# A re-costed order for the first pass of a Mamba-style block, with x_proj's weights filled up to a full 128 x 128

## The chip, the cores and the metric

The kernel runs on one core of a Trainium2 chip. The metric is the device time of one execution in microseconds. Before the change it is 10,700.71 us, the median of three runs (10,697.7 to 10,703.4). The profile used here is of one execution whose span is 10,692.9 us.

## The reference, cut to what matters

Input `x` is 8 images of 64 x 64 tokens with 96 channels (L = 4096 tokens each). The first layer is a group norm and a selective-scan block; after it come a linear attention and a quantized feed-forward layer. What the change touches is all ahead of the scan:

```python
xz = einsum('bhwc,ec->bhwe', group_norm(x), in_proj_w)         # 96 -> 192 + 192 channels
xin, z = split(xz, 2)
xc = silu(conv3x3_depthwise(xin) + conv_b)                     # 192 channels, 64 x 64
x_hw, x_wh = xc.reshape(b, 192, L), xc.transpose(0, 1, 3, 2).reshape(b, 192, L)
xs = stack([x_hw, x_wh, flip(x_hw), flip(x_wh)])               # 4 directions
x_dbl = einsum('bkdl,kcd->bkcl', xs, x_proj_weight)            # 192 -> 6 + 16 + 16 per direction
dts, Bs, Cs = x_dbl[:, :, :6], x_dbl[:, :, 6:22], x_dbl[:, :, 22:]
delta = softplus(dt_w @ dts + dt_bias);  y = selective_scan(xs, delta, A, Bs, Cs)
```

The forward and the flipped direction of one reading order share their input, so one product with 2 x 38 = 76 output rows serves both.

## The kernel before, in words

The program is three passes, one after the other, with tensors in memory between them.

**Pass 1** (`pass1`) takes the images in four pairs. For each image, `statistics` loads x in groups of 512 tokens, transposes it on TensorE (4 transposes of 128 tokens) and collects means on VectorE. `group_norm` makes the scale from two tiny matmuls with `gmat`. `projection` loads and transposes the group again, normalizes it on VectorE (`xn`), and multiplies it by three weights of 96 rows x 128 columns (`pa`); ScalarE copies the results to the padded images `xpad` and applies SiLU to the gates `z`. `convolution` does the nine taps of the depthwise 3 x 3 convolution on VectorE over 128 x 4096 elements. 192 channels are no multiple of 128, so a pair makes three convolutions: channels 0 to 127 of each image, and one tile with the last 64 channels of both images (rows 0 to 63 of the first, 64 to 127 of the second). They run in the order 0, 2, 1. ScalarE then writes SiLU once in transposed order (`ut`, stored to `u_d`) and once in place (`u`).

`x_projection(b, o, q)` multiplies 512 positions of an image by `w_xp`. With o = 0 the positions are adjacent in `u`; with o = 1 they are read in the transposed order, 64 elements apart. Each unit has two matmuls that add in one PSUM tile: 128 rows of the image's own tile, then the 64 rows which belong to the image in the shared one. Each fp32 matmul shows as two passes in the trace, so a unit is four passes. 128 units make up the pass. ScalarE (or VectorE, for half of the last pair's groups) evacuates 76 x 512 to `xd`, and SyncE's queue stores it. `split` reads part of that back, cuts it into three bf16 parts by turns of a ScalarE cast and a GpSimd subtraction, and stores them for pass 2. There are six such units per image.

**Pass 2** does the scans, and **pass 3** the rest. The change leaves both as they are.

What sets the order: `weave` holds a list of generators. Each one yields the engine that its next instructions go to, a cost, a delay until the result is there, and where it matters a set of buffers (`Slots`). `weave` always takes the piece that can begin first by these numbers, and emits its instructions. `InOrder` then keeps each engine, SyncE's DMA queue too, in exactly that order. The costs put no wait into the program; they only choose the order. An instruction whose data is late holds up everything behind it on its engine. All instructions emitted through `InOrder` carry line 89 in the profile, so they are told apart by tile names.

Of the kernel before, what the change touches and what calls it, by code (L numbers as in the profile page):

```python
# [33 lines left out]
F32 = mybir.dt.float32  # L34
# [5 lines left out]
PSUM = bass.MemoryType.PSUM  # L40
DRAM = bass.MemoryType.DRAM

P = 128
NB, HH, WW, C = 8, 64, 64, 96
L = HH * WW
DI, N, R, K = 192, 16, 6, 4
# [27 lines left out]
def load_by_type(queue, dst, src):  # L74

    queue.dma_start(dst[:, 0], src[0:P])
    queue.dma_start(dst[0:64, 1], src[P:DI])
    queue.dma_start(dst[64:P, 1], src[P:DI])
# [154 lines left out]
def pass1(ctx, tc, g, consts, ident, mhalf, engines, u_d, z_d, xd_d, b_d, dt_d):  # L233
# [8 lines left out]
    four = ctx.enter_context(tc.tile_pool(name="p1four", bufs=4))  # L242
    ps_tr = ctx.enter_context(tc.tile_pool(name="p1tr", bufs=2, space=PSUM))
    ps_mm = ctx.enter_context(tc.tile_pool(name="p1mm", bufs=3, space=PSUM))
    ps_px = ctx.enter_context(tc.tile_pool(name="p1px", bufs=2, space=PSUM))
    ps_one = ctx.enter_context(tc.tile_pool(name="p1ps", bufs=1, space=PSUM))
    Q = GRP // P

    ORDER = (0, 2, 1)
# [9 lines left out]
    act.dma_start(gmat, g["group_mean"])  # L259
    conv_w = wp.tile([P, 2, 9], F32, name="conv_w")  # L260
    conv_b = wp.tile([P, 2, 1], F32, name="conv_b")
    w_xp = wp.tile([P, 2, 2, 2 * NXD], F32, name="w_xp")

    def later_loads():
        load_by_type(act, conv_w, g["conv_w"])
        load_by_type(act, conv_b, g["conv_b"])
        w0 = 0
        for rows in (slice(R, R + N), slice(R + N, NXD), slice(0, R)):
            wide = rows.stop - rows.start
            for k2 in range(2):  # L270
                src = slice(k2 * NXD + rows.start, k2 * NXD + rows.stop)
                load_by_type(act, w_xp[:, :, :, w0 : w0 + wide], g["x_projT"][:, :, src])
                w0 += wide


# [5 lines left out]
        pool.memset(t[:, 1 : HH + 1, WW + 1 : WW + 2], 0.0)  # L281

    sts, gms, us, done = {}, {}, {}, {}
    pts, mms, pxs = Slots(2), Slots(3), Slots(2)
    counts = {}

    def one_more(key, of, end):
# [14 lines left out]
    def statistics(b, q):  # L302
        if b > 1:
            yield "proj", b - 2
        yield "sp", 0.5, 2.0
        x = transposed(three, "xs", b, q)
        next(x)
        yield "pe", 0.7, 0.3, pts
        pt, slot = next(x), pts.taken
        end = yield "dve", 0.7  # L310
        if b not in sts:
            sts[b] = two.tile([C, NG, 6], F32, name="st")
        dve.bn_stats(sts[b][:, q, :], pt[0:C, :])
        pts.release(slot, end)
        one_more(("st", b), NG, end)

    def group_norm(b):

        yield "st", b
        yield "dve", 0.2  # L320
        mv = two.tile([C, 2], F32, name="mv")
        dve.bn_aggr(mv, sts[b].rearrange("p a b -> p (a b)"))
        yield "pe", 0.3
        pm = ps_one.tile([P, 2], F32, name="pm", tag="pm")
        pe.matmul(pm[0:C, 0:1], gmat, mv[:, 0:1], start=True, stop=True)
        yield "dve", 0.5
        gm = wp.tile([C, 2], F32, name=f"gm{b}")
        dve.tensor_copy(gm[:, 0:1], pm[0:C, 0:1])
        dq = two.tile([C, 1], F32, name="dq")
        dve.tensor_sub(dq, mv[:, 0:1], gm[:, 0:1])  # L330
        dve.scalar_tensor_tensor(dq, dq, dq, mv[:, 1:2], ALU.mult, ALU.add)
        yield "pe", 0.3
        pv = ps_one.tile([P, 2], F32, name="pv", tag="pm")
        pe.matmul(pv[0:C, 0:1], gmat, dq, start=True, stop=True)
        yield "dve", 0.2
        dve.tensor_copy(gm[:, 1:2], pv[0:C, 0:1])
        end = yield "pool", 1.0
        pool.tensor_scalar(gm[:, 1:2], gm[:, 1:2], 1e-5, None, ALU.add)
        pool.tensor_tensor(gm[:, 1:2], gm[:, 1:2], mhalf[0:C, 0:1], ALU.pow)
        gms[b] = gm  # L340
        done["stats", b] = end

    def projection(b, q):

        pair, j = b // 2, b % 2
        cols = slice(q * GRP, (q + 1) * GRP)
        rows = slice(1 + q * RPG, 1 + (q + 1) * RPG)
        inner = slice(1, WW + 1)
        own, other = slice(64 * j, 64 * j + 64), slice(64 - 64 * j, P - 64 * j)
        third = xpad[2 + pair % 2]  # L350
        yield "stats", b
        yield "sp", 0.5, 2.0
        x = transposed(four, "xt", b, q)
        next(x)
        if pair > 0:
            yield "conv", pair - 1, j
        if pair > 1:
            yield "conv", pair - 2, 2
        yield "pe", 0.7, 0.3, pts
        pt, slot = next(x), pts.taken  # L360
        end = yield "dve", 0.7
        pts.release(slot, end)
        xn = four.tile([C, GRP], F32, name="xn")
        dve.tensor_scalar(xn, pt[0:C, :], gms[b][:, 0:1], gms[b][:, 1:2], ALU.subtract, ALU.mult)
        def product(w):
            yield "pe", 1.1, 0.3, mms
            p = ps_mm.tile([P, GRP], F32, name="pa", tag="mm")
            pe.matmul(p, w, xn, start=True, stop=True)
            return p, mms.taken

        pa, slot = yield from product(w_in[:, 0:P])
        end = yield "act", 0.6
        act.copy(xpad[j][:, rows, inner], pa.rearrange("p (h w) -> p h w", w=WW))
        mms.release(slot, end)
        pa, slot = yield from product(w_mix[:, j, :])
        yield "act", 0.6
        act.copy(third[own, rows, inner], pa[own, :].rearrange("p (h w) -> p h w", w=WW))
        z1 = three.tile([P, GRP], F32, name="z1")
        end = yield "act", 0.6
        act.activation(z1[other, :], pa[other, :], AF.Silu)  # L380
        one_more(("proj", b), NG, end)
        mms.release(slot, end)
        pa, slot = yield from product(w_in[:, DI : DI + P])
        z0 = three.tile([P, GRP], F32, name="z0")
        end = yield "act", 0.6
        act.activation(z0, pa, AF.Silu)
        mms.release(slot, end)
        yield "sp", 0.9
        sp.dma_start(z_d[b][P:DI, cols], z1[other, :])
        sp.dma_start(z_d[b][0:P, cols], z0)  # L390

    def convolution(pair, c):
# [28 lines left out]
            yield "stored", *before  # L421
        parts = chunk_rows(pair, c)
        for w in (slice(i, i + WW // 4) for i in range(0, WW, WW // 4)):
            yield "act", 1.2
            ut = two.tile([P, L // 4], F32, name="ut")
            act.activation(ut.rearrange("p (w h) -> p h w", h=HH), uv[:, :, w], AF.Silu, bias=conv_b[:, ty, :])
            yield "sp", 0.5
            for part, b, ch in parts:
                sp.dma_start(u_d[b][1][ch, w.start * HH : w.stop * HH], ut[part, :])
        for h in range(2):  # L430
            cols = slice(h * (L // 2), (h + 1) * (L // 2))
            end = yield "act", 1.9
            act.activation(u[:, cols], u[:, cols], AF.Silu, bias=conv_b[:, ty, :])
        done["u", pair, c] = end
        end = yield "sp", 0.5
# [3 lines left out]

    def x_projection(b, o, q):  # L440
        pair, j = b // 2, b % 2
        half = slice(64 * j, 64 * j + 64)
        yield "u", pair, j
        yield "u", pair, 2
        px = None
        for ty, u, part in ((0, us[pair, j], slice(0, P)), (1, us[pair, 2], half)):
            end = yield ("pe", 0.85) if px else ("pe", 0.85, 0.3, pxs)
            if px is None:
                px, slot = ps_px.tile([P, GRP], F32, name="px", tag="px"), pxs.taken
            if o == 0:  # L450
                src = u[part, q * GRP : (q + 1) * GRP]
            else:
                src = u[part, :].rearrange("p (h w) -> p w h", w=WW)[:, q * RPG : (q + 1) * RPG, :]
            pe.matmul(px[0 : 2 * NXD, :], w_xp[part, ty, o, :], src, start=ty == 0, stop=ty == 1)
        one_more(("xproj", b), 2 * NG, end)
        by_dve = pair == NB // 2 - 1 and q % 2 == 1
        end = yield ("dve" if by_dve else "act"), 0.6
        xd = three.tile([2 * NXD, GRP], F32, name="xd")
        (dve.tensor_copy if by_dve else act.copy)(xd, px[0 : 2 * NXD, :])
        pxs.release(slot, end)  # L460
        end = yield "sp", 0.5, 2.5
        sp.dma_start(xd_d[b][o][:, q * GRP : (q + 1) * GRP], xd)
        one_more(("xd", b, o), NG, end)

    def split(b, o, row, rows, pieces, at, dst):

        wide, used = GRP, rows * pieces
        yield "xd", b, o
        yield "sp", 0.5, 2.5
        bq = three.tile([P, wide], F32, name="bq")  # L470
        src = xd_d[b][o][row : row + rows].rearrange("r (s t) -> (r s) t", s=pieces)
        sp.dma_start(bq[0:used], src[:, at : at + wide])
        yield "act", 0.6
        bs = three.tile([P, NS, wide], BF16, name="bs")
        act.copy(bs[0:used, 0, :], bq[0:used])
        yield "pool", 1.2
        pool.tensor_sub(bq[0:used], bq[0:used], bs[0:used, 0, :])
        yield "act", 0.6
        act.copy(bs[0:used, 1, :], bq[0:used])
        yield "pool", 1.2  # L480
        pool.tensor_sub(bs[0:used, 2, :], bq[0:used], bs[0:used, 1, :])
        yield "sp", 0.9
        half = used // 2
        for k2 in range(2):
# [612 lines left out]
```

## Time and profile before

| view | what it gives |
| --- | --- |
| span, busy share | 10,692.9 us; VectorE 90%, ScalarE 87%, GpSimd 86%, TensorE 73% |
| first convolution tap of each pair | 74.8, 240.3, 441.9 and 653.8 us |
| end of the last convolution tap | 859.3 us |
| last x_proj matmul starts | 937.4 us |
| first VectorE instruction of pass 2 | 983.5 us |
| convolution taps in all, VectorE | 96 x 4,590 ns and 12 x 2,531 ns, together 471 us |
| x_proj passes, TensorE | 512, mean 929 ns of one |

From about 1,000 us on, VectorE, ScalarE and GpSimd are all over 90% busy. The first 980 us look otherwise: no engine is busy all the time. A share of busy time over the whole span hides this, so the profile has to be read by stage. [...]how long one really holds the engine is seen from the distance between starts in a dense stretch.

### The profile page before, as it was taken

How to read it: one execution, taken by the hardware profiler on the slowest of the kernel's cores; microseconds unless marked ns; L12 is line 12 of the kernel's file. 1: busy time of each engine (PE TensorE's matmuls, PEld its weight loads, DVE VectorE, ACT ScalarE, POOL GpSimd, SP SyncE). 2: the span in 40 equal slices, each digit the busy share in tenths (PEclk: the TensorE clock that was granted, in tenths of full speed). 3: DMA queues.
4: the chain of work that ended last, by engine and by line, in shares of the span. 5: the costliest groups of instructions: out<-in, count | busy, mean ns of one | idle time of the engine just before them, and what ended most of it. 6: DMA issues, size and time to landing. Idle time of an engine off the chain costs nothing.

```text
span 10692.9 us, 151366 instructions
## 1 busy us (share of the span) xinstructions
PE 7776.9 (73%) x51232; PEld 6178.1 (58%) x51232; DVE 9619.3 (90%) x6982; ACT 9298.7 (87%) x21355; POOL 9181.8 (86%) x3270
## 2 busy tenths in 40 slices
PE   6876777777767777777777777777777777766887
PEld 3222656666656666665656666665565666655766
DVE  6664999999999999999999999999999999997776
ACT  4445999999999999999999999999999999996665
POOL 1324999999999999999999999999999999997886
PEclk8777999998899999999899999988999999897776
DMA  5555666669896666689976766789766667997442
GB/s 145 170 165 168 211 217 216 210 211 204 197 210 215 210 219 213 213 205 203 200 218 210 222 211 214 208 200 204 216 210 215 217 207 214 199 198 184 135 128 59
DMA packets 928009, 2103.22 MB, mean 197 GB/s; under 512 B 274391, under 2 KB 422648, under 8 KB 925700
## 3 DMA queue, kind: packets, MB, share of 16 engines
q1 hardware_dynamic: 919812, 2092.79, 69.6%
q8 instruction: 410, 6.72, 0.3%
q14 instruction: 363, 2.97, 0.1%
q10 hardware_dynamic: 7424, 0.74, 0.1%
HBM read 1917.59 MB, written 175.66 MB: 196 GB/s over the span
## 4 chain that ended last, share of the span: by engine, by line
ACT 28%; DVE 20%; PE 17%; issue 17%; POOL 13%; DMA 4%; SPq 1%; ACTq 0%; DVEq 0%; POOLq 0%
DVE h L89 15%; ACT x L89 13%; ACT da L89 10%; POOL c L89 9%; PE wide L89 6%; PE acc L89 6%; DVE wide L89 3%; PE px L89 2%; PE mm L89 2%; ACT L89 1%; POOL xg L89 1%; PE pa L89 1%; ACT delta L89 1%; DMA xdt<-dt_d 1%; SPq L89 1%
## 5 line engine op out<-in xcount | busy, mean ns | idle before, releaser
L89 POOL TENSOR_TENSOR c<-c,h 128x2048 f32<-128x2048 f32 x1536 | 6965.6, 4549 | 395.8 <-DVE h L89 335.4
L89 DVE TENSOR_TENSOR_SCAN h<-da,carry,wide 128x1024 f32<-128x1024 f32 x2304 | 5253.5, 2331 | 204.4 <-PE wide L89 147.4
L89 ACT ACTIVATE x<-duT,bT 128x128 f32<-128x128 f32 (+1 forms) x14336 | 4155.2, 366 | 63.5 <-PE wide L89 57.5
L89 PE MATMUL acc<-ident,c 128*128 128x128 f32 x24576 | 3480.5, 297 | 546.6 <-POOL c L89 539.6
L89 ACT ACTIVATE da<-delta,a_neg 128x1024 f32<-128x1024 f32 x3072 | 3504.2, 1144 | 345.6 <-DVE h L89 333.9
L89 PEld LDWEIGHTS acc<-ident,c 128*128 128x128 f32 x24576 | 3133.3, 155 | 881.1 <-POOL c L89 747.9
L89 PE MATMUL wide<-ident,x 128*128 128x128 f32 x11264 | 1614.0, 292 | 877.9 <-DVE h L89 861.0
L89 PEld LDWEIGHTS wide<-ident,x 128*128 128x128 f32 x11264 | 1344.9, 149 | 1171.7 <-DVE h L89 509.3
L89 DVE TENSOR_TENSOR_SCAN h<-da,wide 128x1024 f32<-128x1024 f32 x768 | 1707.0, 2270 | 82.8 <-PE wide L89 62.0
L89 DVE TENSOR_TENSOR wide<-du,wide 128x1024 f32<-128x1024 f32 x1216 | 1459.2, 1212 | 156.9 <-PE wide L89 156.8
L89 PE MATMUL wide<-xb,sel 96*128 96x512 bf16 x2432 | 752.4, 394 | 584.9 <-DVE h L89 494.7
L89 POOL TENSOR_TENSOR xg<-duT,bT 128x512 f32<-128x512 f32 (+1 forms) x640 | 891.4, 1408 | 82.3 <-PE wide L89 65.1
L89 PE MATMUL wide<-ident,xg 128*128 128x128 f32 x3584 | 500.2, 285 | 239.6 <-DVE h L89 233.7
L89 PEld LDWEIGHTS <-sel 96*128 96x128 bf16 x2432 | 223.0, 101 | 776.0 <-DVE h L89 387.3
L89 PEld LDWEIGHTS wide<-ident,xg 128*128 128x128 f32 x3584 | 412.6, 146 | 316.0 <-issue 143.9
L89 POOL TENSOR_TENSOR du<-delta,u 128x1024 f32<-128x1024 f32 x192 | 455.0, 2370 | 101.4 <-ACT delta L89 92.2
L89 ACT ACT_TABLE_LOAD x385 | 494.0, 1283 | 6.8
L89 PE MATMUL px<-u,w_xp 128*76 128x512 f32 (+1 forms) x512 | 409.5, 929 | 76.5 <-ACT xd L89 47.8
L89 POOL TENSOR_TENSOR bq<-bq,bs 128x512 f32<-128x512 f32 (+1 forms) x48 | 114.2, 2392 | 401.3 <-ACT bs L89 401.2
L89 DVE SCALAR_TENSOR_TENSOR u<-xpad,conv_w,u 128x4096 f32<-128x4096 f32 x96 | 440.6, 4590 | 1.2
L89 PEld LDWEIGHTS px<-u,w_xp 128*76 128x76 f32 (+1 forms) x512 | 78.8, 190 | 364.4 <-issue 217.2
L89 ACT COPY xd<-px 76x512 f32<-76x512 f32 x112 | 65.2, 583 | 254.8 <-PE px L89 169.9
(130 smaller groups left out, 6224.0 us busy)
## 6 DMA issues: line engine op xcount, KB each, us to landing
c<-xd_d SPq DMA_DIRECT2D x1024, 1024.0 KB
c<-xd_d SPq DMA_DIRECT2D x1024, 512.0 KB
u<-u_d SPq DMA_DIRECT2D x128, 512.0 KB
xdt<-dt_d SPq DMA_DIRECT2D x1152, 36.0 KB
xb<-b_d SPq DMA_DIRECT2D x384, 96.0 KB
u<-u_d SPq DMA_DIRECT2D x128, 256.0 KB
y_d<-y SPq DMA_DIRECT2D x24, 1024.0 KB
y<-y_d SPq DMA_DIRECT2D x64, 384.0 KB
```

Source lines behind the costliest of these rows:

```text
L89: ins = getattr(self.engine, op)(*args, **kwargs).ins
```

## The change

It has three parts, all in pass 1.

1. **x_proj's weights.** `w_xp` becomes 128 rows x 3 x 2 x 128 columns, zeroed at the start by GpSimd. Its first block holds the weights of the 128 own channels; the second and third hold those of the last 64 channels in rows 0 to 63 or 64 to 127, with zeros in the other half. Both matmuls of a unit then use all 128 rows of `u` and write 128 columns, 76 of them used. This is meant to spare TensorE the change between 64 and 128 rows and to show it as fully used.
2. **The plan's durations.** Costs and delays given to `weave` are replaced by those that the author read from a trace: a GpSimd subtraction of `split` 4.4 in place of 1.2 (2.5 for the last image but one), `ut` 2.1 in place of 1.2, a product 0.75 in place of 1.1, loads with a delay of 4.0 in place of 2.0 or 2.5, and small ones.
3. **Buffers and engines.** The two tiny group-norm products use the `mm` PSUM tiles, so that x_proj has three PSUM tiles in place of two. The subtractions of the last image go to VectorE.

```diff
-    ps_px = ctx.enter_context(tc.tile_pool(name="p1px", bufs=2, space=PSUM))
-    ps_one = ctx.enter_context(tc.tile_pool(name="p1ps", bufs=1, space=PSUM))
+    ps_px = ctx.enter_context(tc.tile_pool(name="p1px", bufs=3, space=PSUM))
...
-    w_xp = wp.tile([P, 2, 2, 2 * NXD], F32, name="w_xp")
+    w_xp = wp.tile([P, 3, 2, P], F32, name="w_xp")
+    pool.memset(w_xp, 0.0)
...
-                load_by_type(act, w_xp[:, :, :, w0 : w0 + wide], g["x_projT"][:, :, src])
+                act.dma_start(w_xp[:, 0, :, w0 : w0 + wide], g["x_projT"][0:P, :, src])
+                for j in range(2):
+                    act.dma_start(w_xp[64 * j : 64 * j + 64, 1 + j, :, w0 : w0 + wide], g["x_projT"][P:DI, :, src])
...
-    pts, mms, pxs = Slots(2), Slots(3), Slots(2)
+    pts, mms, pxs = Slots(2), Slots(3), Slots(3)
...
-        yield "sp", 0.5, 2.0
+        yield "sp", 0.6, 4.0
...
-        yield "pe", 0.3
-        pm = ps_one.tile([P, 2], F32, name="pm", tag="pm")
+        yield "pe", 0.3, 0.3, mms
+        pm, slot = ps_mm.tile([P, GRP], F32, name="pm", tag="mm"), mms.taken
...
-            yield "pe", 1.1, 0.3, mms
+            yield "pe", 0.75, 0.4, mms
...
-            yield "act", 1.2
+            yield "act", 2.1
...
-        for ty, u, part in ((0, us[pair, j], slice(0, P)), (1, us[pair, 2], half)):
-            end = yield ("pe", 0.85) if px else ("pe", 0.85, 0.3, pxs)
+        for ty, u in ((0, us[pair, j]), (1 + j, us[pair, 2])):
+            end = yield ("pe", 0.9, 0.4) if px else ("pe", 0.9, 0.4, pxs)
...
-            pe.matmul(px[0 : 2 * NXD, :], w_xp[part, ty, o, :], src, start=ty == 0, stop=ty == 1)
+            pe.matmul(px, w_xp[:, ty, o, :], src, start=ty == 0, stop=ty > 0)
...
-        end = yield "sp", 0.5, 2.5
+        end = yield "sp", 0.9, 3.0
         sp.dma_start(xd_d[b][o][:, q * GRP : (q + 1) * GRP], xd)
...
+        name, cost, by = ("dve", 0.65, dve) if b == NB - 1 else ("pool", 4.4 if b < NB - 2 else 2.5, pool)
         yield "xd", b, o
-        yield "sp", 0.5, 2.5
+        yield "sp", 0.7, 4.0
...
-        yield "pool", 1.2
-        pool.tensor_sub(bq[0:used], bq[0:used], bs[0:used, 0, :])
+        yield name, cost
+        by.tensor_sub(bq[0:used], bq[0:used], bs[0:used, 0, :])
```

More of the change, by code (lines that the diff above doesn't have):

```diff
@@ L322, in group_norm @@
         dve.bn_aggr(mv, sts[b].rearrange("p a b -> p (a b)"))
-        yield "pe", 0.3
-        pm = ps_one.tile([P, 2], F32, name="pm", tag="pm")
+        yield "pe", 0.3, 0.3, mms
+        pm, slot = ps_mm.tile([P, GRP], F32, name="pm", tag="mm"), mms.taken
         pe.matmul(pm[0:C, 0:1], gmat, mv[:, 0:1], start=True, stop=True)
-        yield "dve", 0.5
+        end = yield "dve", 0.5
+        mms.release(slot, end)
         gm = wp.tile([C, 2], F32, name=f"gm{b}")
@@ L331, in group_norm @@
         dve.scalar_tensor_tensor(dq, dq, dq, mv[:, 1:2], ALU.mult, ALU.add)
-        yield "pe", 0.3
-        pv = ps_one.tile([P, 2], F32, name="pv", tag="pm")
+        yield "pe", 0.3, 0.3, mms
+        pv, slot = ps_mm.tile([P, GRP], F32, name="pv", tag="mm"), mms.taken
         pe.matmul(pv[0:C, 0:1], gmat, dq, start=True, stop=True)
-        yield "dve", 0.2
+        end = yield "dve", 0.2
+        mms.release(slot, end)
         dve.tensor_copy(gm[:, 1:2], pv[0:C, 0:1])
@@ L351, in projection @@
         yield "stats", b
-        yield "sp", 0.5, 2.0
+        yield "sp", 0.6, 4.0
         x = transposed(four, "xt", b, q)
@@ L360, in projection @@
         pt, slot = next(x), pts.taken
-        end = yield "dve", 0.7
+        end = yield "dve", 0.8
         pts.release(slot, end)
@@ L431, in convolution @@
             cols = slice(h * (L // 2), (h + 1) * (L // 2))
-            end = yield "act", 1.9
+            end = yield "act", 2.0
             act.activation(u[:, cols], u[:, cols], AF.Silu, bias=conv_b[:, ty, :])
@@ L441, in x_projection @@
         pair, j = b // 2, b % 2
-        half = slice(64 * j, 64 * j + 64)
         yield "u", pair, j
@@ L450, in x_projection @@
             if o == 0:
-                src = u[part, q * GRP : (q + 1) * GRP]
+                src = u[:, q * GRP : (q + 1) * GRP]
             else:
-                src = u[part, :].rearrange("p (h w) -> p w h", w=WW)[:, q * RPG : (q + 1) * RPG, :]
-            pe.matmul(px[0 : 2 * NXD, :], w_xp[part, ty, o, :], src, start=ty == 0, stop=ty == 1)
+                src = u.rearrange("p (h w) -> p w h", w=WW)[:, q * RPG : (q + 1) * RPG, :]
+            pe.matmul(px, w_xp[:, ty, o, :], src, start=ty == 0, stop=ty > 0)
         one_more(("xproj", b), 2 * NG, end)
@@ L475, in split @@
         act.copy(bs[0:used, 0, :], bq[0:used])
-        yield "pool", 1.2
-        pool.tensor_sub(bq[0:used], bq[0:used], bs[0:used, 0, :])
+        yield name, cost
+        by.tensor_sub(bq[0:used], bq[0:used], bs[0:used, 0, :])
         yield "act", 0.6
         act.copy(bs[0:used, 1, :], bq[0:used])
-        yield "pool", 1.2
-        pool.tensor_sub(bs[0:used, 2, :], bq[0:used], bs[0:used, 1, :])
+        yield name, cost
+        by.tensor_sub(bs[0:used, 2, :], bq[0:used], bs[0:used, 1, :])
         yield "sp", 0.9
```

## The prediction

> **What bounds the kernel now.** I read the page first: over the whole span VectorE is busiest (90%), but the change touches pass 1 alone, so I took the busy time of each engine in 100-us stretches. The columns are PE, PEld, DVE, ACT and POOL busy, then the granted clock, the DMA share and GB/s.
>
> ```profile
> 400.00:500.00 100.00, 78.57 (x102) 19.31 (x100) 61.91 (x21) 36.26 (x54) 57.84 (x20) 0.57 0.42 119
> 600.00:700.00 100.00, 78.83 (x105) 16.97 (x104) 56.31 (x16) 33.17 (x48) 44.70 (x18) 0.58 0.47 131
> 900.00:1000.00 100.00, 52.39 (x135) 18.66 (x134) 21.31 (x17) 35.01 (x70) 28.82 (x17) 0.66 0.50 150
> 1000.00:1100.00 100.00, 73.28 (x560) 62.83 (x559) 96.67 (x51) 97.47 (x217) 93.96 (x25) 0.95 0.66 213
> ```
>
> Pass 2 (last line) is full on three engines. In pass 1 none is full; TensorE is the busiest, at a clock that falls to 0.57. Next the waits of the first 960 us, and those of SyncE's queue:
>
> ```profile
> DVE xn L89 <- PE pt L89: 156.0, 32, 31.1
> PE pt L89 <- DMA xt<-in_x: 56.2, 18, 7.6
> PEld px L89 <- ACT xd L89: 92.5, 42, 9.8
> ...
> SPq L89 <- ACT xd L89: 171.5, 69, 6.9
> SPq L89 <- POOL bs L89: 100.2, 18, 14.4
> ```
>
> VectorE waits for TensorE; TensorE for loads and for evacuations; the queue that issues those loads stands up to 14.4 us behind one GpSimd subtraction. The timelines of TensorE and VectorE show it at one place:
>
> ```profile
> 451.78 23.07 PE L89 MATMUL px<-u,w_xp 128*76 128x512 f32 x24 [2.77 <-ACT xd L89]
> 474.78 1.94 PE L89 MATMUL pt<-ident,xt 128*96 128x128 f32 x8
> ...
> 441.92 3.25 DVE L89 TENSOR_SCALAR u<-xpad,conv_w 128x4096 f32<-128x4096 f32 x1
> 475.98 1.59 DVE L89 TENSOR_SCALAR xn<-pt,gm 96x512 f32<-96x512 f32 x2 [30.81 <-PE pt L89]
> ```
>
> VectorE has one tap left to give and then stands 30.8 us, since `xn` is next in its order and its transpose lies behind the x_proj passes. The same recurs at 657 us (31.1 us). So pass 1 is set by order: x_proj's slow stretches on TensorE, with VectorE idle beside them.
>
> [...]from 447 to 474 us PE is busy 24.2 of 27 us, yet the clock is 0.50. A dense stream of 76-column passes does not hold the clock; dense 96x128 products do from 52 to 90 us. [...]adjacent passes of one form at full clock start 0.43 us apart, and 0.52 where 128 and 64 rows change. [...]o = 1 passes (elements 256 bytes apart) start 0.86 us apart even where the clock is 1.00 (919.4 to 922.6 us). [...]Here one GpSimd subtraction takes 1.15 us alone and up to 6.1 us beside the convolution, against 1.2 in the old plan.
>
> **The change, part by part.**
>
> *Weights, row changes.* In `749.19 9.06 ... x18` (full clock, adjacent reads, rows changing) a pass is 9.06/18 = 0.50 us, in the 24 strided passes above 0.96. Without changes 0.43 and 0.86. A strided unit goes from 3.84 to 3.43 us: 64 x 0.41 = 26 us. A plain unit at full clock goes from 2.01 to 1.72: by the single records, 87 of some 250 plain passes run at half clock, about 22 of 64 units, so 42 at full: 42 x 0.29 = 12 us.
>
> *Weights, clock.* The other 22 plain units run at half clock, some 3.7 us each. If full columns and rows count as busy, they fall to 1.72: 22 x 2.0 = 44 us. No row of this trace shows a 128x128 fp32 pass of 512 columns; the bounds are 22 x 0.3 = 7 us (clock unchanged) and 44 us, and I take 44, since 96x128 products hold the clock. Projections gain too: their 384 passes average 0.71 and 0.70 us against 0.59 at full clock, an excess of 45 us, of which I take a third, 15 us. The strided passes gain nothing from the clock, as they are as slow at 1.00 as at 0.50. TensorE in sum: 26 + 12 + 44 + 15 = 97 us of 711 busy before 960 us. Wider weight loads cost nothing: the 128-column loads of `pa` (225 ns for `px`'s 190) lie under the passes before them. Zeroing `w_xp` on GpSimd lies in its idle start (16 us idle until 17.6 us), ahead of the loads issued from 37.9 us on; their number stays 18.
>
> *How much of it reaches the end.* From 230 to 650 us PE is busy 344 of 420 us and VectorE 278, so TensorE sets the pace, and VectorE is the next limit: a convolution of 2.35 + 8 x 4.4 = 37.6 us plus its share of `xn` and statistics, the first two starting 49 and 50 us apart. 47 x 12 = 564 us after 75 us gives about 640 us for the last tap, against 859. The 97 us fit in this gap of 220, so I count them whole.
>
> *Order.* With 4.4 for a subtraction, the casts behind it on ScalarE and the stores behind it on SyncE come later in the order, with `xd` copies and x loads ahead of them. That goes for the 100 us of queue waits on `bs`, and part of the 92.5 us that loads of x_proj wait for `xd`. The third PSUM tile for x_proj helps the latter. From 230 to 860 us PE idles 141 us; I take 55, about half of the queue's wait for `bs`. Bounds: 0 (only other places to wait) and 110. The new waits of `pm` and `pv` for an `mm` tile hold, on TensorE, everything behind them, until ScalarE has evacuated a product (0.6 us each): 16 of them, under 10 us in all, beside VectorE's taps.
>
> *Tail.* From the last tap (859.3) to pass 2's first VectorE instruction (983.5) are 124 us: SiLU 28 with waits, x_proj until 938, then 45 for the last split and pass 2's first loads. After: SiLU 4 x 2.08 + 2 x 2.0 = 12, say 15; 16 units, 8 x 1.72 + 8 x 3.43 = 41; the 45 stay. That is 101, or 23 less, of which half is counted above: 10 us. The last image's 12 subtractions on VectorE, some 0.7 us each by its copies, are not more than on GpSimd.
>
> Sum: 97 + 55 + 10 = 162 us. 10,701 - 162 = 10,539, rounded to 10,540. Passes 2 and 3 stay: their order is planned from a clock of its own.
>
> **The rivals.** *VectorE's floor:* the plan comes out so well that convolutions follow each other at 47 us. Last tap at 640, tail 101: pass 2 starts at 741, 242 us earlier: about 10,450. For it: GpSimd, ScalarE and SyncE all have room. Against: every engine is in fixed order, and load waits of 4 to 8 us remain. *Row changes only:* the clock stays low and the new order only moves waits: 26 + 12 + 7 = 45 and a few us of the tail: 10,650. [...]*A worse order:* the same products, but wrong costs (0.9 for strided matmuls, which take 1.7) let the plan put transposes and group norm behind x_proj; five more holds like that at 442 us, 5 x 31 = 155, less the 97 and 10 that remain, some 48 us slower: 10,750. For it: the plan is blind to o. Against: it was as blind before (0.85).
>
> **How the numbers follow.** Forecast 0.60, VectorE's floor 0.15, row changes only 0.15, a worse order 0.06, and 0.04 for gains and losses that cancel. The range goes from VectorE's floor, 10,450, to just short of the row-change case, 10,640. Faster takes the first three: 0.90; same 0.04; slower 0.06.
>
> **What would show it.** In the changed profile x_proj passes should start 0.43 (plain) and 0.86 us (strided) apart with no 0.52; clock in the stretches 400 to 700 us above 0.75; the wait of `xn` for `pt` well under 156 us; SyncE's wait for `bs` under 50; last tap near 720, pass 2's first VectorE instruction near 820 us. The prediction is wrong if strided passes also speed up, if the clock stays near 0.57, or if `xn` waits longer than before.

## The result and the profile after

The changed kernel takes 10,573.22 us (median, 10,562.6 to 10,580.3) against 10,702.06 us for the kernel before in the same comparison: a ratio of 0.9876, 95% interval 0.9859 to 0.9893. That is 129 us less. The prediction was 10,540 us, 162 us less, with a range of 10,450 to 10,640. The direction and the range hold. The experiments below show that the sum behind it does not: the term for the weights is several times too large, the term for the order half of what the order gave.

All of it comes from pass 1. The first VectorE instruction of pass 2 starts at 853.4 us instead of 983.5, which is 130 us. The busy time in 100-us stretches (PE, PEld, DVE, ACT and POOL busy, then granted clock, DMA share, GB/s), kernel after:

```profile
400.00:500.00 100.00, 91.17 (x229) 36.20 (x228) 78.67 (x36) 68.59 (x96) 55.31 (x14) 0.98 0.73 234
600.00:700.00 100.00, 63.88 (x117) 22.05 (x118) 90.76 (x25) 59.42 (x70) 63.59 (x17) 0.83 0.62 204
```

VectorE has gone from 62 to 79 us in the stretch from 400 us and from 56 to 91 in the one from 600 us; the clock there rose from 0.57 and 0.58 to 0.98 and 0.83. The waits of the first 840 us (waiter, releaser, us in total, times, longest):

```profile
DVE xn L89 <- PE pt L89: 58.3, 23, 11.4
PE pt L89 <- DMA xt<-in_x: 19.3, 12, 4.5
PEld px L89 <- ACT xd L89: 39.5, 31, 5.7
```

and those of SyncE's queue in the same time:

```profile
SPq L89 <- ACT xd L89: 180.7, 77, 8.9
SPq L89 <- POOL bs L89: 17.6, 9, 3.8
```

`xn` waits 58 us for its transposes instead of 156, and SyncE's queue 18 us for GpSimd's subtractions of the split instead of 93 in the same 840 us (100 in the first 960; another 9 us now go to the subtractions that VectorE does). The long hold at the start of a pair, 30.8 us before, is still there but shorter, 11.4 us. TensorE and VectorE after, at the same point of the third pair:

```profile
388.99 22.39 PE L89 MATMUL px<-u,w_xp 128*128 128x512 f32 x28
411.20 1.05 PE L89 MATMUL pt<-ident,xt 128*96 128x128 f32 x8
...
398.15 2.35 DVE L89 TENSOR_SCALAR u<-xpad,conv_w 128x4096 f32<-128x4096 f32 x1
411.93 1.52 DVE L89 TENSOR_SCALAR xn<-pt,gm 96x512 f32<-96x512 f32 x2 [11.43 <-PE pt L89]
```

The last tap ends at 731.9 us (before 859.3). From there to pass 2's first VectorE instruction it is still 121.5 us (before 124.2).

### The profile page after: what moved, and what is told of

Same layout as the page of the kernel before. It is cut to its first block, busy times and chain, and to the rows that moved or that the text cites. A ratio compares the mean times of both kernels' runs of the same rounds, so it can differ in the third digit from the quotient of the medians.

```text
span 10564.6 us, 151369 instructions
## 1 busy us (share of the span) xinstructions
PE 7682.5 (73%) x51232; PEld 6188.4 (59%) x51232; DVE 9627.7 (91%) x6994; ACT 9296.5 (88%) x21355; POOL 9255.5 (88%) x3259
## 4 chain that ended last, share of the span: by engine, by line
ACT 28%; DVE 21%; PE 18%; issue 17%; POOL 12%; DMA 3%; SPq 1%; DVEq 0%; ACTq 0%; POOLq 0%
DVE h L89 15%; ACT x L89 13%; ACT da L89 10%; POOL c L89 9%; PE wide L89 6%; PE acc L89 6%; DVE wide L89 3%; PE px L89 2%; PE mm L89 2%; ACT L89 1%; POOL xg L89 1%; DVE u L89 1%; PE pa L89 1%; ACT delta L89 1%; ACT duT L89 1%
## 5 line engine op out<-in xcount | busy, mean ns | idle before, releaser
L89 POOL TENSOR_TENSOR xg<-duT,bT 128x512 f32<-128x512 f32 (+1 forms) x640 | 891.6, 1408 | 79.7 <-PE wide L89 60.6
L89 PE MATMUL px<-u,w_xp 128*128 128x512 f32 x512 | 368.4, 869 | 68.7 <-ACT u L89 45.0
L89 PE MATMUL mm<-w_out,gt 128*128 128x96 f32 (+1 forms) x1024 | 267.1, 382 | 32.8 <-POOL gt L89 16.9
L89 PEld LDWEIGHTS px<-u,w_xp 128*128 128x128 f32 x512 | 106.2, 215 | 273.3 <-issue 170.4
```

The costliest lines, as they stand in the source:

```text
L89: ins = getattr(self.engine, op)(*args, **kwargs).ins
```

## The experiments

Times are compared by their ratio to the kernel before, run on the same chip in the same comparison; that kernel's median was 10,702.6, 10,706.3 and 10,699.4 us in the three comparisons. "Half-clock time" is the sum of the clock records at 0.50 from 45 us to the last x_proj matmul: 475 us before, 167 us after. It is read, like every view, from one execution of each kernel. In the changed kernel at full clock, a pass over adjacent elements lasts 0.59 us in the trace, yet the next one starts 0.43 us after its start: their records overlap, so what a pass costs is taken from the starts.

### The weights alone, and the plan alone

Theory A is the prediction's sum, TensorE's saving counted whole and the order on top. Theory B is that the order pays. Theory C is that the weights are all of it. The first kernel puts only this into the kernel before:

```diff
-    w_xp = wp.tile([P, 2, 2, 2 * NXD], F32, name="w_xp")
+    w_xp = wp.tile([P, 3, 2, P], F32, name="w_xp")
+    pool.memset(w_xp, 0.0)
...
-            pe.matmul(px[0 : 2 * NXD, :], w_xp[part, ty, o, :], src, start=ty == 0, stop=ty == 1)
+            pe.matmul(px, w_xp[:, ty, o, :], src, start=ty == 0, stop=ty > 0)
```

> The kernel before with the weights filled up to 128 x 128 alone; plan, buffers and engines as before. Theory A (the prediction's sum): TensorE's saving counts whole, 85 to 105 us faster, so about 10,605. Theory B (it is the order that pays): the old order cannot use a faster TensorE, under 45 us faster, 10,660 or more. Theory C (the weights are all): about 129 us faster, 10,573. In each, half-clock time in pass 1 falls from 475 us to under 250 us.

The second takes the changed kernel and puts just those lines back.

> The changed kernel with the old weights and matmuls (76 columns, 128 and 64 rows); new costs, buffers and engines stay. Theory A: 35 to 55 us faster than before, about 10,655. Theory B: 80 to 129 us faster, 10,575 to 10,620. Theory C: within 20 us of before. Under A and B SyncE's queue waits for the split's subtractions under 50 us instead of 100.

Measured: weights alone 10,674.83 us, ratio 0.9974 (0.9964 to 0.9984), 28 us faster. Plan alone 10,586.01 us, ratio 0.9893 (0.9877 to 0.9910), 117 us faster. Theory B holds and A and C fall. To see what happened on TensorE, take each kernel from its start to the end of its last x_proj pass. All of them run the same 1,440 matmul passes in that time. The lines give TensorE's busy time (the first number after the length), in the order kernel before, weights alone, plan alone, changed kernel:

```profile
0.00:938.40 938.40, 707.83 (x1440) 232.31 (x1440) 578.61 (x304) 401.45 (x533) 237.80 (x128) 0.75 0.54 158
0.00:916.30 916.30, 651.61 (x1440) 257.14 (x1440) 578.12 (x304) 401.31 (x533) 230.08 (x129) 0.84 0.54 162
0.00:830.70 830.70, 670.55 (x1440) 221.26 (x1440) 589.54 (x309) 401.02 (x533) 296.67 (x122) 0.82 0.60 178
0.00:807.80 807.80, 622.16 (x1440) 247.45 (x1440) 588.61 (x309) 400.62 (x533) 318.38 (x123) 0.90 0.60 183
```

| kernel | last x_proj pass ends, us | TensorE busy, us | TensorE idle, us | half-clock time, us |
| --- | --- | --- | --- | --- |
| before | 938.4 | 707.8 | 230.6 | 475 |
| weights alone | 916.3 | 651.6 | 264.7 | 290 |
| plan alone | 830.7 | 670.6 | 160.2 | 300 |
| changed | 807.8 | 622.2 | 185.6 | 167 |

The weights alone take 56 us of work from TensorE, but its last x_proj pass ends only 22 us earlier: the other 34 us came back as idle time. The half-clock time fell to 290 us, less far than expected (under 250). The waits of the first 960 us of the weights-alone kernel:

```profile
PEld px L89 <- ACT xd L89: 117.7, 51, 11.2
PE px L89 <- ACT xd L89: 74.9, 20, 10.4
...
DVE xn L89 <- PE pt L89: 143.2, 28, 30.9
```

Before the change the first two rows were 92.5 and 47.8 us. The second, of the matmuls themselves, has grown by 27 us, most of the 34. (The first is of the weight loads. In the kernel before, passes of TensorE ran during 44.6 of their 92.5 us of waiting, so the two rows must not be added.) For the most part TensorE only reaches sooner the point where an evacuation has to come first. `xn` still waits 143 us, and the hold in the same place is 28.8 us:

```profile
443.71 20.95 PE L89 MATMUL px<-u,w_xp 128*128 128x512 f32 x24 [4.91 <-ACT xd L89]
464.48 1.05 PE L89 MATMUL pt<-ident,xt 128*96 128x128 f32 x8
...
465.21 1.53 DVE L89 TENSOR_SCALAR xn<-pt,gm 96x512 f32<-96x512 f32 x2 [28.83 <-PE pt L89]
```

In the plan-alone kernel SyncE's queue waits 14 us for GpSimd's subtractions, although every x_proj pass has the same rows and columns as before. The plan does two things. TensorE idles 70 us less. It is also 37 us less busy with the same passes, and its half-clock time falls from 475 us to 300: the plan alone raises the clock. So not all of the changed kernel's clock is owed to the weights. Busy time from 200 to 700 us, as the sum over five stretches of 100 us and their mean, in the order kernel before, weights alone, plan alone, changed kernel:

```profile
sum 500.00, PE 408.90 PEld 127.09 DVE 314.98 ACT 222.61 POOL 157.03; mean PE 81.78 PEld 25.42 DVE 63.00 ACT 44.52 POOL 31.41
```

```profile
sum 500.00, PE 371.60 PEld 142.44 DVE 323.26 ACT 230.59 POOL 162.52; mean PE 74.32 PEld 28.49 DVE 64.65 ACT 46.12 POOL 32.50
```

```profile
sum 500.00, PE 444.58 PEld 136.00 DVE 389.52 ACT 271.19 POOL 233.43; mean PE 88.92 PEld 27.20 DVE 77.90 ACT 54.24 POOL 46.69
```

```profile
sum 500.00, PE 409.82 PEld 156.08 DVE 411.38 ACT 285.34 POOL 277.74; mean PE 81.96 PEld 31.22 DVE 82.28 ACT 57.07 POOL 55.55
```

The weights alone lower PE's busy time by 37 us of 500 and give VectorE only 8. The plan alone raises VectorE by 75 us, with TensorE at 89%. On top of the plan the weights lower PE again and give VectorE 22 more; up to the last x_proj pass they take another 48 us of work away, of which 25 come back as idle time.

### Rows or columns

Two kernels fill up one side of the weights only, in the kernel before. The first asks whether full columns alone raise the clock; the estimate for that case was that most of the 475 us of half-clock time would go, and some 60 us of time with it (10,640). Columns:

```diff
-    w_xp = wp.tile([P, 2, 2, 2 * NXD], F32, name="w_xp")
+    w_xp = wp.tile([P, 2, 2, P], F32, name="w_xp")
+    pool.memset(w_xp, 0.0)
...
-            pe.matmul(px[0 : 2 * NXD, :], w_xp[part, ty, o, :], src, start=ty == 0, stop=ty == 1)
+            pe.matmul(px, w_xp[part, ty, o, :], src, start=ty == 0, stop=ty == 1)
```

> The kernel before with w_xp's columns alone filled up to 128; rows still change between 128 and 64. [...]if it is the rows and the changes between them, half-clock time stays above 400 us and the time within 20 us of before.

Rows:

```diff
-    w_xp = wp.tile([P, 2, 2, 2 * NXD], F32, name="w_xp")
+    w_xp = wp.tile([P, 3, 2, 2 * NXD], F32, name="w_xp")
+    pool.memset(w_xp, 0.0)
...
-            pe.matmul(px[0 : 2 * NXD, :], w_xp[part, ty, o, :], src, start=ty == 0, stop=ty == 1)
+            pe.matmul(px[0 : 2 * NXD, :], w_xp[:, ty, o, :], src, start=ty == 0, stop=ty > 0)
```

> The kernel before with rows alone filled up to 128; 76 columns. No changes of row form are left: the two passes of a strided unit start 0.86 us apart. If rows set the clock, half-clock time falls to under 250 us and the time to about that of the weights alone; if columns do, it stays above 350 us and only the row changes are saved, 20 to 40 us.

Columns alone: 10,701.95 us, ratio 1.0000 (0.9992 to 1.0009), half-clock time 520 us. Rows alone: 10,683.15 us, ratio 0.9983 (0.9975 to 0.9991), half-clock time 277 us. The same dense stretch of 24 strided passes, timeline of TensorE, first with columns filled, then with rows filled:

```profile
452.76 24.11 PE L89 MATMUL px<-u,w_xp 128*128 128x512 f32 x24 [3.07 <-ACT xd L89]
```

```profile
444.49 20.84 PE L89 MATMUL px<-u,w_xp 128*76 128x512 f32 x24 [3.66 <-ACT xd L89]
```

And the busy time and clock in those stretches, in the same order (columns as above, the clock is the first number after POOL):

```profile
447.00:474.00 27.00, 23.93 (x25) 5.99 (x24) 0.00 (x0) 7.20 (x13) 6.79 (x6) 0.50 0.39 119
```

```profile
443.00:470.00 27.00, 24.97 (x46) 6.93 (x46) 4.11 (x3) 11.65 (x16) 6.78 (x6) 0.94 0.45 142
```

With 128 columns and changing rows the clock stays at 0.50. With 76 columns and constant rows it is 0.94 (0.93 over the strided passes alone, 444.5 to 465.3 us; the stretch shown takes in a few others at its end). So filling up the columns did not raise the clock here. The 277 us of half-clock time are somewhat more than expected if rows set the clock (under 250), and rows alone and the whole weights differ by less than their intervals tell apart. Nor do changing rows always mean a low clock: the plan-alone kernel has them too, and 300 us. Filling up rows does two things at once: all 128 rows are used, and the row form no longer changes between matmuls. Which of the two the higher clock goes with was not separated.

### Which part of the plan

Theory S is that the cost of the split's subtraction is what pays, theory D that the gain is spread. One kernel takes this entry alone into the kernel before:

```diff
-        yield "pool", 1.2
+        yield "pool", 4.4 if b < NB - 2 else 2.5
```

> The kernel before with one plan entry changed: a GpSimd subtraction of the split costs 4.4 (2.5 for the last two images) in place of 1.2. Theory S (this one cost is what pays): 70 us or more of the plan's 116 come, 10,630 or less, and SyncE's queue waits for the subtractions under 40 us instead of 93. Theory D (the gain is spread over the costs): under 45 us faster, though the same queue wait falls.

The other puts 1.2 back into the changed kernel.

> The changed kernel with the cost of a GpSimd subtraction put back to 1.2; all else stays. Theory S: 60 us or more slower than the changed kernel, 10,635 or more, with SyncE's wait for the subtractions back at about 90 us. Theory D: within 30 us of the changed kernel, under 10,605.

Alone it gives 10,650.69 us, ratio 0.9951 (0.9934 to 0.9968), 56 us faster. Without it the changed kernel takes 10,671.07 us, ratio 0.9971 (0.9959 to 0.9982): 98 of the 129 us are lost. SyncE's queue in that kernel:

```profile
SPq L89 <- POOL bs L89: 139.9, 21, 19.8
```

and VectorE's hold at the start of the third pair is back:

```profile
449.36 1.53 DVE L89 TENSOR_SCALAR xn<-pt,gm 96x512 f32<-96x512 f32 x2 [32.74 <-PE pt L89]
```

So this entry is necessary for most of the gain, but it isn't enough: with 56 us alone it lies between the 70 that theory S asked for and the 45 that theory D allowed. In the kernel with it alone SyncE waits only 13 us for the subtractions in the first 960 us, yet the hold is shortened rather than gone:

```profile
448.42 1.59 DVE L89 TENSOR_SCALAR xn<-pt,gm 96x512 f32<-96x512 f32 x2 [23.39 <-PE pt L89]
```

Read as in the table above, the entry alone takes away waiting and nothing else: up to the last x_proj pass, which ends at 876.1 us, TensorE is busy 706.3 us, as before, and idle 169.8 us, 61 less; half-clock time is 424 us. Without the entry the changed kernel is back at 647.3 us busy and 267.2 us idle, close to the weights alone, and its time is that of the weights alone too (ratio 0.9971 against 0.9974). So without this entry the rest of the plan adds nothing to the weights that can be measured.

Three kernels look for the partner. The diff shows their main lines, in this order. Each undoes one group of the other edits in the changed kernel: the PSUM tiles; the costs of TensorE and ScalarE; the costs and delays of SyncE.

```diff
-    ps_px = ctx.enter_context(tc.tile_pool(name="p1px", bufs=3, space=PSUM))
+    ps_px = ctx.enter_context(tc.tile_pool(name="p1px", bufs=2, space=PSUM))
+    ps_one = ctx.enter_context(tc.tile_pool(name="p1ps", bufs=1, space=PSUM))
...
-            yield "pe", 0.75, 0.4, mms
+            yield "pe", 1.1, 0.3, mms
...
-            yield "act", 2.1
+            yield "act", 1.2
...
-        yield "sp", 0.6, 4.0
+        yield "sp", 0.5, 2.0
```

> The changed kernel with the PSUM tiles as before: two for x_proj, one for the group norm's tiny products, which then need no mm tile. If the third x_proj tile is part of the plan's gain beyond the split's cost (some 60 us), 15 to 40 us slower than the changed kernel; if the order alone is, within 10 us of it.

> The changed kernel with TensorE's and ScalarE's old costs (product 1.1, x_proj 0.85 with a delay of 0.3, ut 1.2). If the plan needs all its costs right, 20 to 50 us slower than the changed kernel; if the split's subtraction is the one that matters, within 15 us of it.

> The changed kernel with the old costs and delays of SyncE's loads and x_proj's store (0.5 with delays of 2.0 and 2.5). If the plan needs the later landing of loads, 15 to 40 us slower than the changed kernel, with more wait of TensorE for x loads; otherwise within 10 us.

| undone in the changed kernel | us | ratio to the kernel before | interval |
| --- | --- | --- | --- |
| nothing | 10,573.22 | 0.9876 | 0.9859 to 0.9893 |
| PSUM tiles | 10,569.80 | 0.9876 | 0.9859 to 0.9892 |
| TensorE and ScalarE costs | 10,578.78 | 0.9889 | 0.9874 to 0.9903 |
| SyncE costs and delays | 10,579.06 | 0.9888 | 0.9874 to 0.9903 |
| cost of the subtraction | 10,671.07 | 0.9971 | 0.9959 to 0.9982 |

None of the three can be told from the changed kernel. Each group can be spared when the rest is there, and only the subtraction's cost cannot. From the entry alone to the whole plan the last x_proj pass moves 45 us forward; 36 of these are less busy time on TensorE, at 300 us of half-clock time instead of 424, and only 10 less idling. Which of the other edits brings that is not settled: several groups may stand in for each other, or small shifts of the order may add up. No run has the weights with this entry alone.

### The last image's subtractions

The changed kernel with them back on GpSimd:

```diff
-        name, cost, by = ("dve", 0.65, dve) if b == NB - 1 else ("pool", 4.4 if b < NB - 2 else 2.5, pool)
+        name, cost, by = ("pool", 4.4 if b < NB - 2 else 2.5, pool)
```

> The changed kernel with the last image's split subtractions back on GpSimd (cost 2.5). If moving them to VectorE shortened the tail, 5 to 10 us slower than the changed kernel; if they only wait in VectorE's order behind evacuations, as fast or up to 10 us faster.

10,572.42 us, ratio 0.9876 (0.9862 to 0.9891). The move changes nothing that can be measured.

### Reading u without the stride

The strided passes start 0.86 us apart after the change (median of 218 neighbours, all at full clock). Before, that held within one row form at full clock (0.86, 50 neighbours); at half clock it was 0.94 us (89), and where the rows changed 0.96 at full and 0.97 at half. This kernel reads runs of 8 adjacent elements and turns the result in the evacuation:

```diff
-                src = u.rearrange("p (h w) -> p w h", w=WW)[:, q * RPG : (q + 1) * RPG, :]
+                src = u.rearrange("p (h w) -> p h w", w=WW)[:, :, q * RPG : (q + 1) * RPG]
...
-        (dve.tensor_copy if by_dve else act.copy)(xd, px[0 : 2 * NXD, :])
+        out_, in_ = xd, px[0 : 2 * NXD, :]
+        if o == 1:
+            out_, in_ = xd.rearrange("p (w h) -> p w h", h=HH), in_.rearrange("p (h w) -> p w h", w=RPG)
+        (dve.tensor_copy if by_dve else act.copy)(out_, in_)
```

> The changed kernel, but the o = 1 products read u in runs of 8 adjacent elements and leave the turn to the evacuation, which then reads its PSUM tile 8 elements apart. The results are the same. Passes of o = 1 should start 0.43 us apart instead of 0.86: 256 x 0.43 = 110 us less on TensorE. If TensorE still paces pass 1, 50 us or more faster than the changed kernel (under 10,525). If order and the convolutions pace it, only the tail's 8 units count, 8 x 1.7 = 14 us, and part of the short holds: 10,540 to 10,570. A slower evacuation on ScalarE (over 1.2 us for 0.58) would take that back.

10,523.43 us, ratio 0.9830 (0.9815 to 0.9845): about 50 us less than the changed kernel, just at the edge of what was expected if TensorE paces the pass, and 183 us less than the one before. Where 24 strided passes took 20.8 to 24.1 us above, in this kernel's tail 17 take 7.5 us:

```profile
734.72 7.46 PE L89 MATMUL px<-u,w_xp 128*128 128x512 f32 x17
```

Counted from start to start without the idle time, the 256 passes with o = 1 hold TensorE for 119 us instead of 220. Up to the last x_proj pass TensorE is busy 88 us less than in the changed kernel and idle 31 us more. The evacuation pays nothing for the turn; the copies as this kernel's trace has them (shortest, median and longest duration; half of them turn):

```profile
L89 ACT COPY xd<-px x112: 566/581/628, 195.5 to 752.8; 76x512 f32<-76x512 f32 x112
```

The median is 581 ns, as in the kernel before, and so it is for the 56 that turn taken alone. What it waits for most now is a buffer to write to:

```profile
ACT xd L89 <- DMA xd_d<-xd: 79.7, 35, 8.5
```

The last kernel gives `xd` a fourth buffer, and finds the space by leaving `w_xp` at 76 columns, rows filled up.

```diff
-        xd = three.tile([2 * NXD, GRP], F32, name="xd")
+        xd = four.tile([2 * NXD, GRP], F32, name="xd")
...
-    w_xp = wp.tile([P, 3, 2, P], F32, name="w_xp")
+    w_xp = wp.tile([P, 3, 2, 2 * NXD], F32, name="w_xp")
```

> The unstrided kernel (10,523) with four xd buffers in place of three, and w_xp with 76 columns again (rows stay filled up), which frees the space. If columns do nothing, as the two runs on rows and columns say, and ScalarE's 80 us of waits for an xd buffer hold TensorE, 10 to 25 us faster than the unstrided kernel, 10,500 to 10,515; if the columns do hold the clock, half-clock time rises over 300 us and the time over 10,530.

10,526.86 us, ratio 0.9835 (0.9821 to 0.9850): the same as without, where 10 to 25 us less had been expected. The wait for an `xd` buffer fell from 79.7 to 55.9 us, and nothing came of it, so that much of it did not pace the pass. Half-clock time is 205 us with 76 columns against 222 with 128: a second sign that full columns did not raise the clock.

## Why the prediction was right, and where its steps were not

**Right: what bounded pass 1.** The prediction read the hold at 442 us as order: `xn` behind x_proj passes, loads behind a subtraction that the plan had put at 1.2 us. In the kernel before, six such subtractions in a row take GpSimd 28 us (from 418 to 446 us); SyncE's queue stands behind them until 438 us, and two evacuations then wait 5.7 and 6.7 us for stores of that queue. The two runs on the entry show what it is worth. Alone it ends most of SyncE's wait and shortens the hold from 30.8 to 23.4 us; taken out of the changed kernel, it brings both back.

**Wrong size: the order, 55 us.** The plan alone gives 117. As less idling the term was near: TensorE idles 61 us less with the one entry and 70 us less with the whole plan, of which 55 had been counted. What the prediction put at nothing is that a better order also saves TensorE work. With the old weights, half-clock time falls from 475 to 300 us and the same passes keep TensorE busy 37 us less.

**Wrong step: "The 97 us fit in this gap of 220, so I count them whole."** Both halves of it fail. The saving of work was 56 us with the weights alone and 48 on top of the plan, not 97; the 86 us that the changed kernel saves contain the plan's own share. And it does not arrive whole: the weights alone give 28 us of time, and the plan has 13 left for them (117 against 129, within the intervals' width). PE was 82% busy and VectorE 66%, and the prediction took the busier engine for the one that sets the pace. But TensorE idled too, for loads and for evacuations that had their own place in the order, and when its work shrank, part of the saving became more of that idling: 34 us in the old order, 25 us in the new one. The rival "row changes only" came nearer to the weights' effect, 45 for 28, but for another reason: it expected the clock to stay low, and the clock rose.

**Wrong in part: the columns.** The 44 us for the clock rested on "if full columns and rows count as busy", an assumption that no trace had shown. The clock did rise, but with 76 columns as well as with 128 (half-clock time 277 us with rows alone, 290 with the whole weights, 475 before), so filling up the rows was enough. The prediction's own lines spoke against "A dense stream of 76-column passes does not hold the clock": its 18 passes at 749 us have 76 columns and run at full clock (granted clock 1.00 from 749.2 to 758.3 us). The strided passes start 0.858 us apart in the changed kernel, as foretold, and all 256 of them ran at full clock, against the rival "row changes only", in which the clock stays low. That they were "as slow at 1.00 as at 0.50" was not so in the kernel before, where they were 0.94 us apart at half clock within one row form; with constant rows, in the weights-alone kernel, it was so (0.858 and 0.859 us).

**Wrong size: the tail, 10 us.** It got 3 us shorter. SiLU was put at 15 us and x_proj at 41. In the trace of the changed kernel the image's products begin 25 us after the last tap, as SiLU's pieces alternate with evacuations that wait for x_proj's passes of the image before, and end 51 us later instead of 41: one evacuation stood behind a late `bq` load and held TensorE for 4.7 us, and for 8.8 of the 51 us the clock stood at 0.50. The last 45 us stayed, as said.

That the total came within 33 us is in good part luck: an overcount of the weights (97 for the 13 to 28 that they give) and of the tail offset the undercount of the order (55 for 117). The checks set out beforehand mostly hold: 0.43 and 0.86 us, the clock, `xn`'s wait, SyncE's wait of 18 us. The last tap came at 732 for 720 and pass 2 at 853 for 820; 21 of these 33 us are the tail.

## What to carry to other kernels

In a program whose engines run a written order, ask of the busiest engine what its idle time waits for before counting work saved on it as time. In the old order 56 us less work on TensorE gave 28 us of time; in the new one, taking the stride out of half of x_proj's reads saved 88 us of work and gave 50. About half arrived each time.

One wrong duration in a planner can cost far more than the instruction itself, as what the order has put behind a late instruction is late too: here SyncE's queue stood 100 of the first 960 us behind GpSimd's subtractions. The plan's 1.2 us stood for subtractions that took up to 6.1 us beside the convolution, and 1.16 us (median of 56) while VectorE did nothing. Correcting that entry alone gave 56 us and taking the correction out of the changed kernel cost 98. The other edits of the plan gave nothing without it, about 60 us together with it, and could be taken back one group at a time for next to nothing.

A change of order can also change what the work itself costs, so the two must be measured apart: with the matmuls left as they were, the new plan cut TensorE's busy time by 37 us.

## What the runs showed of the hardware that was not expected

- Columns of weights filled up with zeros did not raise the granted clock (half-clock time 520 us against 475), whereas filling up rows, which also ends the changes of row form, did (277 us). In one stretch with full columns TensorE was busy 23.9 of 27 us and the clock still 0.50.
- The plan, which leaves rows and columns of every matmul as they were, moved the granted clock about as much as the weights did: half-clock time 300 us with the plan alone, 290 with the weights alone, 475 before.
- Strided fp32 passes with constant rows start 0.858 us apart at full clock and 0.859 at half (medians in the weights-alone kernel, where 24 of them took 20.95 us in a stretch with a mean clock of 0.88). In the changed kernel all 256 ran at full clock.
- A ScalarE copy of 76 x 512 fp32 out of PSUM takes the same 581 ns read in turn as read 8 elements apart, and a TensorE pass that reads runs of 8 adjacent elements, 64 apart, starts 0.43 us after the one before it (17 passes in 7.46 us), like a fully adjacent one at full clock (0.43 us in the changed kernel).
